# Two small steps of every layer norm move from GpSimd to VectorE in a four-layer graph kernel

## The chip, the cores and the metric

The kernel runs on one core of one Trainium2 chip. A core has TensorE (PE in the profile, with its weight loads apart as PEld), VectorE (DVE), ScalarE (ACT) and GpSimd (POOL), which work from queues of their own and meet by semaphores, and SyncE (SP), whose queue issues nearly all of the DMAs here. The metric is the time of one execution on the device, in microseconds (us); the run is judged by the median of several.

## The reference: four pre-norm graph layers

The input x holds 64 graphs of 256 nodes with 128 features, all with one 256 x 256 adjacency matrix. Every layer does `h = relu(layernorm(x))`, runs a graph layer on h and adds its result to x.

```python
def _layernorm(x, axis=-1, eps=1e-5):
    m = jnp.mean(x, axis=axis, keepdims=True)
    v = jnp.var(x, axis=axis, keepdims=True)
    return (x - m) / jnp.sqrt(v + eps)
...
pre = s1[:, :, None, :] + s2[:, None, :, :] + b_lin
h = jnp.where(pre >= 0, pre, ALPHA * pre)
e = jnp.einsum('bije,e->bij', h, a) + bias
attn = jax.nn.softmax(e, axis=2)
```

The lines from `pre` on are layer 0, the costly one: for every pair of nodes of a graph 256 numbers are made, passed through a leaky relu and summed with weights. Layer 1 is a gated sum over neighbours with two dense steps, layer 2 an attention masked by the adjacency matrix, layer 3 a gated recurrent unit of five steps.

The layer norm is done on all 128 features of a node, so mean and variance are two numbers per node. As nodes lie on the partitions, they are two columns per block of 128 nodes. The kernel never makes the normalized values by themselves: ScalarE computes `relu(rstd * x + shift)` in one instruction, with `rstd = (variance + epsilon) ** -0.5` and `shift = -mean * rstd`.

## The kernel before

**Tiles and groups.** The 64 graphs go in 34 groups: one graph each in the first two and the last two, two graphs in the others (`GROUPS`). A graph is two blocks of 128 nodes, so a group's x is a tile `xt` of 128 partitions by G blocks of 128 features, with G = 2 or 4.

**The layer norm** is `ln_relu` (L445 to L481), and every group goes through it four times, once per layer, 136 times in all. VectorE makes the statistics of each block (`bn_stats`, L457, into `bst`) and joins them (`bn_aggr`, L460, into `bmv`, which holds mean and variance side by side per block). Then GpSimd does four instructions on tiles of G columns: `bve` = variance + epsilon (L465), `bmm` = -mean (L466), `brs` = `bve` to the power -0.5 (L468) and `bsh` = `bmm` x `brs` (L470). Then ScalarE makes h, block by block (L477), with `bsh` and `brs` as its bias and scale. The generator yields the name of an engine ahead of each step; what stands between two yields is queued on that engine in one go.

**The pair stage** of layer 0 is most of the work. For each graph, `Pairs` makes buffers `r` of 128 x 4 x 2 x 256, in which a tile of 256 columns is the maximum of s2 and one column of -s1. Three engines make such tiles, each in its own form: ScalarE (L720, a relu with a bias), GpSimd (L725, one tile per instruction, all in SBUF) and VectorE (L702, four or eight tiles in one instruction, s2 read from PSUM and s1n from SBUF). A full buffer is a batch; TensorE sums it with the weights into `e_ps` (L786), and the buffer is free again. There are 12 buffers. When five or more batches wait for TensorE, the planner "merges": VectorE adds two buffers into one (L744, a maximum and a sum in one instruction), so that TensorE gets three batches in place of four.

**The order of the work** is set when the kernel is built, by a planner in the last part of the function. It keeps a clock for each of the four engines (`Model`), to which every instruction adds a price written in the code: a tile 365 ns on ScalarE and 454 on GpSimd, a VectorE instruction of the pair stage 1131, 2198 or 392, and for small ones

```python
def dve(n, pointers=0, more=0):
    model.op("dve", 66 + n * 1.042 + 60 * pointers + more)
    return nc.vector
def pool(ns):
    model.op("pool", ns)
    return nc.gpsimd
```

At each turn it takes the piece of work that can start first by these clocks: a step of one of the chains (layer norms and dense layers of other groups, each a generator), a batch for TensorE, a merge, or tiles for an engine that is free. A step that follows one on another engine may start 150 to 300 ns after it (`LAG`), and 100 ns more for most (300 for TensorE) while chains are paced. So a change of one price changes the order of nearly all of the program, and how many tiles each engine is given. On the chip every engine keeps the order it was given, whatever the instructions take in fact.

**Other places that the prediction speaks of.** At the start some constants are made on VectorE: L252 to L274 put the attention weights into order, L338 to L340 work on columns of two (`left`, `left_n`, `left_nb`), L442 adds two biases. L815 is the reciprocal of layer 0's softmax. L800 joins scores with adjacency and takes a minimum, L870 is layer 1's elu.

Of the kernel before, what the change touches and what calls it, by code (L numbers as in the profile page):

```python
# [8 lines left out]
F32 = mybir.dt.float32  # L9
AF = mybir.ActivationFunctionType  # L10
ALU = mybir.AluOpType

P = 128
N = 256
GROUPS = (1, 1) + (2,) * 30 + (1, 1)
LN_EPS = 1e-5
# [49 lines left out]
def kernel(ctx: ExitStack, tc: tile.TileContext, ins: dict, out: bass.AP):  # L66
# [9 lines left out]
    sp = ctx.enter_context(tc.tile_pool(name="small", bufs=3))  # L76
# [31 lines left out]
# [4 lines that stand above are left out]
    def act(n, pointers=0, sbuf=0, table=0, more=0):  # L112
        model.op("act", 50 + n * 0.832 + 69 * sbuf + (0, 75, 154)[pointers] + 11 * table + more)
        return nc.scalar
# [4 lines that stand above are left out]
# [329 lines left out]
    def ln_relu(space, xt, tag, ln, when=None, at=None, across=False):  # L448

        G = xt.shape[1]  # L450
        for g in range(G):
            if g % 2 == 0:
                yield "dve", when, at
            if g == 0:
                st = sp.tile([P, G, 6], F32, tag=tag + "_st", name="bst", bufs=1)
                mv = sp.tile([P, G, 2], F32, tag=tag + "_mv", name="bmv", bufs=1)
            dve(P).bn_stats(st[:, g, :], xt[:, g, :])  # L457
        yield "dve"
        for g in range(G):
            dve(6, more=15).bn_aggr(mv[:, g, :], st[:, g, :])  # L460
        yield "pool"

        ve = sp.tile([P, G], F32, tag=tag + "_ve", name="bve", bufs=1)
        minus = sp.tile([P, G], F32, tag=tag + "_mm", name="bmm", bufs=1)
        pool(277).tensor_scalar(ve, mv[:, :, 1], 1.0, LN_EPS, ALU.mult, ALU.add)  # L465
        pool(150).tensor_scalar(minus, mv[:, :, 0], -1.0, 0.0, ALU.mult, ALU.add)  # L466
        rstd = sp.tile([P, G], F32, tag=tag + "_rs", name="brs", bufs=1)
        pool(1085).tensor_tensor(rstd, ve, neg_half[:, 0:G], ALU.pow)  # L468
        shift = sp.tile([P, G], F32, tag=tag + "_sh", name="bsh", bufs=1)
        pool(302).tensor_tensor(shift, minus, rstd, ALU.mult)  # L470
        for g in range(G):
            if g % 2 == 0:
                yield "act"
            if g == 0:
                shape = [P, P, G] if across else [P, G, P]
                h = space.tile(shape, F32, tag=ln, name=tag, bufs={ap: 3, bp: 1}.get(space))
            act(P, 2, 1).activation(  # L477
                h[:, :, g] if across else h[:, g, :], xt[:, g, :], AF.Relu, bias=shift[:, g : g + 1],
                scale=rstd[:, g : g + 1],
            )  # L480
        return h  # L481
# [15 lines left out]
    def first_head(xt, to, snd):  # L497

        G, _, W = sizes(xt)
        h = yield from ln_relu(ap, xt, "h0", "h0", at=LANDS)  # L500
        h_t = yield from transpose_blocks(ap, h, "h0t", psum_h)
        to.update(h=h, h_t=h_t)
        yield "pe", lambda: counts["w_p"] > 1
        s2_ps, s1_ps = psum_h([P, 2, N], "s2_ps"), psum_a([P, 2, W], "s1_ps")
        for half, p in ((1, s2_ps), (0, s1_ps)):
            for ec in range(2):
                mm(
                    p[:, ec, :], lhsT=w_p[:, half, bass.ts(ec, P)], rhs=flat(h_t),
                    start=True, stop=True,
                )  # L510
        yield "dve"
        s1n = ap.tile([P, 2, W], F32, tag="s1n", name="s1n")
        for ec in range(2):
            dve(W, 1).tensor_scalar(
                s1n[:, ec, :], s1_ps[:, ec, :], -1.0, blin_n[:, ec : ec + 1], ALU.mult, ALU.add
            )
        yield "act"
        s2 = ap.tile([P, 2, N], F32, tag="s2", name="s2")
        act(2 * N).copy(s2, s2_ps)
        s1 = ap.tile([P, 2, W], F32, tag="s1", name="s1")  # L520
        for ec in range(2):
            act(W, 1, more=27).activation(
                s1[:, ec, :], s1_ps[:, ec, :], AF.Identity, bias=blin_p[:, ec : ec + 1]
            )
        to.update(s1=s1, s1n=s1n)
        snd.update(s2=s2, s2_ps=s2_ps)

    def head(xt, to):
        G, _, W = sizes(xt)
        h = yield from ln_relu(ap, xt, "h0", "h0")  # L530
        h_t = yield from transpose_blocks(ap, h, "h0t", psum_h, settled)
        to.update(h=h, h_t=h_t)
        if counts["left"] > 0:
            yield from bounds(to)
        for ec in range(2):
            yield "pe", lambda: counts["w_p"] > 0
            p = psum_h([P, W], "s1_ps")
            mm(
                p, lhsT=w_p[:, 0, bass.ts(ec, P)], rhs=flat(h_t), start=True, stop=True
            )  # L540
            yield "act", lambda: counts["w_p"] > 1
            if ec == 0:
                s1 = ap.tile([P, 2, W], F32, tag="s1", name="s1")
                s1n = ap.tile([P, 2, W], F32, tag="s1n", name="s1n")
            act(W, 1, more=27).activation(s1[:, ec, :], p, AF.Identity, bias=blin_p[:, ec : ec + 1])
            yield "act"
            act(W, 1, more=27).activation(
                s1n[:, ec, :], p, AF.Identity, bias=blin_n[:, ec : ec + 1], scale=-1.0
            )
        to.update(s1=s1, s1n=s1n)  # L550
# [432 lines left out]
    def layer2(x2, by_memory):  # L983
        G, NB, W = sizes(x2)
        h = yield from ln_relu(bp, x2, "h2", "h", across=True)
        if by_memory:
            h_t, at = crossed(h, "h_t", "h_t", "act")
# [484 lines left out]
```

## Time and profile before

| | |
|---|---|
| median of 3 runs | 4956.28 us (4955.85 to 4961.9) |
| profiled execution, its own time | 4962.75 us |
| its span, first to last instruction | 4960.9 us |
| granted TensorE clock, mean | 0.999 |
| instructions on VectorE, GpSimd | 8229, 10545 |
| GpSimd tiles, L725 | 9920, busy 4509.6 us, 543 ns each |
| ScalarE tiles, L720 (main group) | 9768, busy 4421.0 us, 1212 ns each |
| VectorE, L702 whole and half | 761 at 2277 ns, 606 at 1210 ns |
| VectorE merges, L744 | 4056 at 472 ns |
| statistics, L457 and L460 | 512 at 278 ns, 512 at 153 ns |

A profile comes from one execution, taken by the hardware profiler. In its groups the first number after the bar is the time in which at least one instruction of the group ran, then the mean time of one, then the idle time of the engine just before them with what ended most of it. Instructions of one engine overlap: a tile of ScalarE shows 1212 ns, yet 9768 of them fit in 4421.0 us. So the time that one more instruction adds to a full engine is less than the time it shows, and is read from runs of equal instructions. TensorE's busy time is modelled, and an engine that is busy in the profile may still wait inside. The last 161 us, after 4800, are a tail in which the last groups end their chains and the makers of tiles have little left.

### The profile page before, as it was taken

To read this page: it belongs to the slowest core of one execution; us is meant where nothing else is said; L and a number is where in the kernel's file an instruction comes from. 1 tells how busy PE (TensorE), PEld (TensorE's weight loads), DVE (VectorE), ACT (ScalarE), POOL (GpSimd) and SP (SyncE) were. 2 spreads that over 40 slices of the span, in tenths; PEclk is the share of its full clock that TensorE was granted. 3 is DMA by queue.
4 is the path that set the end of the run, shared out by engine and by line. 5 is a ranking of instruction groups with operands and counts; after the bars stand their busy time and mean duration, and the time that the engine had idled before them with its cause. 6 is when DMAs were issued, how large, how long until landed. Compare 5 with 4: busy or idle time off the path is not lost.

```text
span 4960.9 us, 176723 instructions
## 1 busy us (share of the span) xinstructions
PE 4923.5 (99%) x69735; PEld 2389.7 (48%) x69735; DVE 4841.8 (98%) x8229; ACT 4873.2 (98%) x12812; POOL 4756.8 (96%) x10545
## 2 busy tenths in 40 slices
PE   9999999999999999999999999999999999999998
PEld 4454545554454544444445444444454444444444
DVE  9999999999999999999999999999999999999994
ACT  8999999999999999999999999999999999999994
POOL 8999999999999999999999999999999999999981
PEclk9999999999999999999999999999999999999999
DMA  0357576777676776866757656656666555542310
GB/s 21 10 17 23 25 30 27 32 32 30 30 33 27 32 32 28 34 27 30 33 27 30 30 27 32 32 26 32 30 32 32 26 31 30 29 26 12 19 9 8
DMA packets 3431090, 132.92 MB, mean 27 GB/s; under 512 B 3369201, under 2 KB 3405937, under 8 KB 3430257
## 3 DMA queue, kind: packets, MB, share of 16 engines
q1 hardware_dynamic: 3429712, 121.35, 56.5%
q8 instruction: 547, 8.96, 0.9%
q14 instruction: 287, 2.34, 0.3%
q10 hardware_dynamic: 544, 0.26, 0.0%
HBM read 61.48 MB, written 60.10 MB: 25 GB/s over the span
## 4 chain that ended last, share of the span: by engine, by line
PE 85%; ACT 7%; DVE 5%; POOL 1%; issue 1%; DMA 0%; ACTq 0%; DVEq 0%; POOLq 0%
PE e_ps L786 53%; PE gate_ps L128 8%; PE hv_ps L128 5%; ACT r L720 5%; PE m_ps L128 5%; PE s_ps L128 3%; DVE r L702 3%; PE o_ps L128 2%; PE e_ps L128 2%; PE rc_ps L128 1%; POOL r L725 1%; PE rsum_ps L128 1%; DVE r L744 1%; PE e_ps L135 1%; PE th_ps L128 1%
## 5 line engine op out<-in xcount | busy, mean ns | idle before, releaser
L725 POOL TENSOR_SCALAR r<-s,s1n 128x256 f32<-128x256 f32 x9920 | 4509.6, 543 | 47.1 <-PE e_ps L786 21.1
L720 ACT ACTIVATE r<-s_act,s 128x256 f32<-128x256 f32 x9768 | 4421.0, 1212 | 1.1 <-PE e_ps L786 1.0
L786 PE MATMUL e_ps<-r,a_win 128*32 128x256 f32 (+1 forms) x41040 | 3323.2, 464 | 9.1 <-DVE r L702 7.5
L702 DVE TENSOR_TENSOR r<-s_ps,s1n 128x2048 f32<-128x2048 f32 (+1 forms) x1367 | 2417.3, 1804 | 0.0
L786 PEld LDWEIGHTS e_ps<-r,a_win 128*32 128x32 f32 x41040 | 1394.2, 110 | 1603.7 <-issue 825.0
L744 DVE SCALAR_TENSOR_TENSOR r<-s_ps,s1n,r 128x256 f32<-128x256 f32 x4056 | 1671.5, 472 | 0.8 <-POOL r L725 0.3
L477 ACT ACTIVATE h<-xt,bsh,brs 128x128 f32<-128x128 f32 x512 | 417.6, 1318 | 7.5 <-POOL bsh L470 7.5
L720 ACT ACTIVATE r<-s,s 128x256 f32<-128x256 f32 x512 | 319.2, 1416 | 0.0
L128 PE MATMUL m_ps<-adj_q,hn 128*32 128x256 f32 x4096 | 252.1, 380 | 1.6 <-ACT hn L1140 1.6
L128 PEld LDWEIGHTS m_ps<-adj_q,hn 128*32 128x32 f32 x4096 | 160.8, 132 | 89.4 <-issue 25.4
L1192 ACT ACTIVATE gate_ps<-gate_ps,bz 128x512 f32<-128x512 f32 (+1 forms) x140 | 202.5, 1447 | 0.0
L1194 ACT ACTIVATE hv_ps<-hv_ps,bh 128x512 f32<-128x512 f32 (+1 forms) x140 | 200.9, 1435 | 0.0
L1180 ACT ACTIVATE m_ps<-gate_ps,br 128x512 f32<-128x512 f32 (+1 forms) x140 | 194.0, 1386 | 0.0
L1176 ACT COPY m_t<-m_ps 128x512 f32<-128x512 f32 (+1 forms) x140 | 184.7, 1319 | 0.0
L128 PE MATMUL gate_ps<-m_t,t_w_w 128*32 128x512 f32 (+1 forms) x1360 | 174.8, 568 | 0.4 <-ACT m_t L1090 0.3
L128 PE MATMUL hv_ps<-rh,u_th 128*32 128x512 f32 (+1 forms) x1360 | 170.9, 567 | 1.3 <-DVE rh L1103 1.3
L128 PE MATMUL gate_ps<-m_t,w_t 128*32 128x512 f32 (+1 forms) x1360 | 171.1, 568 | 0.6 <-ACT m_ps L1100 0.6
L128 PE MATMUL hv_ps<-m_t,t_w_w 128*32 128x512 f32 (+1 forms) x1360 | 171.0, 567 | 0.0
L809 ACT ACTIVATE pm<-e_ps,nmax 128x256 f32<-128x256 f32 x128 | 145.7, 1138 | 2.4 <-DVE nmax L800 2.4
L128 PE MATMUL gate_ps<-hf,u_t 128*32 128x512 f32 (+1 forms) x1088 | 139.8, 567 | 0.0
L128 PE MATMUL s_ps<-h0t,w_p 128*32 128x256 f32 (+1 forms) x1568 | 138.9, 445 | 0.6 <-ACT h0t L493 0.5
L940 ACT ACTIVATE th_ps<-th_ps,a_src 128x256 f32<-128x256 f32 x128 | 134.8, 1053 | 1.5 <-PE th_ps L128 1.5
(223 smaller groups left out, 4612.8 us busy)
## 6 DMA issues: line engine op xcount, KB each, us to landing
there<-hf SPq DMA_DIRECT2D x104, 256.0 KB
hn<-there SPq DMA_DIRECT2D x104, 256.0 KB
there<-h SPq DMA_DIRECT2D x86, 256.0 KB
h_t<-there SPq DMA_DIRECT2D x60, 256.0 KB
xt<-in_x_dram SPq DMA_DIRECT2D x30, 256.0 KB
out_dram<-xt SPq DMA_DIRECT2D x30, 256.0 KB
h3t<-there SPq DMA_DIRECT2D x26, 256.0 KB
row<-rows SPq DMA_DIRECT2D x128, 0.5 KB
```

Source lines behind the costliest of these rows:

```text
L128: nc.tensor.matmul(out[bass.ts(c, 32)], lhsT=lhsT[:, bass.ts(c, 32)], rhs=rhs, **flags)
L477: act(P, 2, 1).activation(h[:, :, g] if across else h[:, g, :], xt[:, g, :], AF.Relu, bias=shift[:, g : g + 1], scale=rstd[:, g : g + 1],)
L702: nc.vector.tensor_tensor(r[:, 2 * g2 : 2 * g2 + n, :, :], s2[:, ec : ec + 1, :].unsqueeze(1).to_broadcast([P, n, 2, N]), s1n.to_broadcast ...
L720: nc.scalar.activation(r[:, g, ic, :], s2[:, ec, :], AF.Relu, bias=s1[:, ec, i : i + 1])
L725: nc.gpsimd.tensor_scalar(r[:, g, ic, :], s2[:, ec, :], FLT_MAX, s1n[:, ec, i : i + 1], ALU.min, ALU.max,)
L744: nc.vector.scalar_tensor_tensor(r[:, g, ic, :], self.own("dve")[:, 1, :], self.of["s1n"][:, 1, i : i + 1], r[:, g, ic, :], ALU.max, ALU.add,)
L786: nc.tensor.matmul(to, lhsT=a_win[:, sign, 31 - t : 63 - t], rhs=of, start=False, stop=self.over, skip_group_check=True,)
L809: act(N, 1, more=119).activation(pm[:, ic, :], e_ps[:, ic, :], AF.Exp, bias=nmax[:, ic : ic + 1], scale=-1.0, accum_out=rs[:, ic : ic + 1],)
L1176: act(W).copy(m_t, m_ps)
L1180: act(W, 1).activation(m_ps, g_ps, AF.Tanh, bias=br, scale=0.5)
L1192: act(W, 1).activation(g_ps, g_ps, AF.Tanh, bias=bz, scale=0.5)
L1194: act(W, 1).activation(hv_ps, hv_ps, AF.Tanh, bias=bh)
```

## The change

The sum of variance and epsilon, which GpSimd made, is made by VectorE, right behind the aggregates and in the same step. The negative mean is no longer made. GpSimd does the power alone, at its old price of 1085. Then the chain goes back to VectorE for a step of its own, in which one instruction makes the shift out of mean, -1 and `rstd`. The chain of engines in a layer norm was VectorE, GpSimd, ScalarE; it is VectorE, GpSimd, VectorE, ScalarE.

```diff
@@ ln_relu
         yield "dve"
         for g in range(G):
             dve(6, more=15).bn_aggr(mv[:, g, :], st[:, g, :])
+        ve = sp.tile([P, G], F32, tag=tag + "_ve", name="bve", bufs=1)
+        dve(G).tensor_scalar(ve, mv[:, :, 1], 1.0, LN_EPS, ALU.mult, ALU.add)
         yield "pool"
 
-        ve = sp.tile([P, G], F32, tag=tag + "_ve", name="bve", bufs=1)
-        minus = sp.tile([P, G], F32, tag=tag + "_mm", name="bmm", bufs=1)
-        pool(277).tensor_scalar(ve, mv[:, :, 1], 1.0, LN_EPS, ALU.mult, ALU.add)
-        pool(150).tensor_scalar(minus, mv[:, :, 0], -1.0, 0.0, ALU.mult, ALU.add)
         rstd = sp.tile([P, G], F32, tag=tag + "_rs", name="brs", bufs=1)
         pool(1085).tensor_tensor(rstd, ve, neg_half[:, 0:G], ALU.pow)
+        yield "dve"
         shift = sp.tile([P, G], F32, tag=tag + "_sh", name="bsh", bufs=1)
-        pool(302).tensor_tensor(shift, minus, rstd, ALU.mult)
+        dve(G).scalar_tensor_tensor(shift, mv[:, :, 0], -1.0, rstd, ALU.mult, ALU.mult)
         for g in range(G):
             if g % 2 == 0:
                 yield "act"
```

In the changed kernel the sum is L462, the power L466 and the shift L469; lines from L477 on stand one lower (L702 is L701, L720 is L719, L725 is L724, L744 is L743, L786 is L785).

## The prediction

> **What bounds the kernel now.** I read the page's busy shares and its chain of work first, then the busy time by stretch, then the groups kept apart by shape.
>
> ```profile
> PE 4923.5 (99%) x69735; PEld 2389.7 (48%) x69735; DVE 4841.8 (98%) x8229; ACT 4873.2 (98%) x12812; POOL 4756.8 (96%) x10545
> PE 85%; ACT 7%; DVE 5%; POOL 1%; issue 1%; DMA 0%; ACTq 0%; DVEq 0%; POOLq 0%
> ```
>
> ```profile
> 100.00:4800.00 4700.00, 4690.85 (x66507) 2280.72 (x66508) 4659.67 (x7900) 4694.95 (x12358) 4623.27 (x10234) 1.00 0.61 28
> 4800.00:4961.00 161.00, 143.71 (x1970) 68.27 (x1960) 91.58 (x208) 90.84 (x222) 47.62 (x112) 0.97 0.02 7
> ```
>
> The second fence gives, per stretch, its length and then the busy time of PE, PEld, DVE, ACT and POOL. In the 4700 us body no engine rests: VectorE is idle 40.3 us of it (0.9%), GpSimd 76.7, the others under 10. That is the planner's doing: it hands each free engine the next tiles of the pair stage, so four engines fill up together. Work taken from one engine is therefore not time won; it is spread by the planner, and the end goes to whichever engine has most work in fact. A price in the planner that is too low makes its engine the late one. The question is what the two moved instructions cost on VectorE, against what the planner thinks.
>
> **What leaves GpSimd.** From the groups by shape (mean ns of one, then idle before):
>
> ```profile
> L468 POOL TENSOR_TENSOR brs<-bve,neg_half 128x4 f32<-128x4 f32 x120 | 122.4, 1020 | 0.0
> L470 POOL TENSOR_TENSOR bsh<-bmm,brs 128x4 f32<-128x4 f32 x120 | 24.1, 201 | 9.4
> L466 POOL TENSOR_SCALAR bmm<-bmv 128x4 f32<-128x4 f32 x120 | 23.4, 195 | 10.1
> L465 POOL TENSOR_SCALAR bve<-bmv 128x4 f32<-128x4 f32 x120 | 23.3, 195 | 23.7 <-DVE bmv L460 15.4
> ```
>
> Each of the three small ones is 0.20 us plus a gap of some 0.08, as one norm in order of time shows: its instructions start at 2071.20, 2071.48, 2071.63 and 2072.73, the tile before ends at 2071.12, and two tiles after end at 2073.98. Less two tiles of 0.454 the block costs 1.95 us. The power alone, with a gap at each side, is 0.08 + 1.02 + 0.11 = 1.21. So 0.74 us goes per norm (0.84 if all three gaps go), times 136 norms = 101 us (to 114).
>
> **What the planner does with it.** The listing of the two built programs shows the change does what it says: 136 + 136 small instructions come to VectorE, 408 small ones on GpSimd become 136. It also shows how the pair stage is dealt anew: GpSimd 9920 to 10088 tiles; ScalarE's main tile group 9768 to 9712; VectorE's whole halves 761 to 726, half ones 606 to 652, merges 4056 to 4040; TensorE two batches more. Nothing else changes in number. Prices: a GpSimd tile is 4509.6/9920 = 0.454 us. Run on run, VectorE's instructions begin about 0.08 before the last one ends (five L744 took 2.05 us, not 5 x 0.472), so 2.20, 1.13 and 0.39 us. ScalarE: sixteen L720 took 6.80 us at 1.21 each, so 0.37. A batch on TensorE is 0.86 in the chain.
> - GpSimd: -101 + 168 x 0.454 = -101 + 76 = **-25 us** (to -38).
> - ScalarE: -56 x 0.37 = **-21 us**.
> - TensorE: **+1.7 us**.
> - VectorE: -35 x 2.20 + 46 x 1.13 - 16 x 0.39 = -77 + 52 - 6 = **-31 us**, before the 272 added ones.
>
> **What the added instructions cost.** The planner books 66 + 4 x 1.042 = 70 ns each, 19 us in all. The nearest rows are the kernel's own small VectorE instructions:
>
> ```profile
> L338 DVE TENSOR_SCALAR left<-left,odd_all 128x2 f32<-128x2 f32 x1 | 0.4, 429 | 0.0
> L339 DVE TENSOR_SCALAR left_n<-left 128x2 f32<-128x2 f32 x1 | 0.4, 420 | 0.0
> L340 DVE TENSOR_TENSOR left_nb<-left_n,c_L_gnn_b_lin 128x2 f32<-128x2 f32 x1 | 0.4, 406 | 0.0
> ```
>
> ```profile
> L442 DVE TENSOR_TENSOR bz<-c_L_gnn_w_b,c_L_gnn_u_b x1: 143/143/143, 103.1 to 103.1; 128x1 f32<-128x1 f32 x1
> L442 DVE TENSOR_TENSOR br<-c_L_gnn_w_b,c_L_gnn_u_b x1: 257/257/257, 103.4 to 103.4; 128x1 f32<-128x1 f32 x1
> L442 DVE TENSOR_TENSOR bh<-c_L_gnn_w_b,c_L_gnn_u_b x1: 348/348/348, 103.7 to 103.7; 128x1 f32<-128x1 f32 x1
> ```
>
> ```profile
> L815 DVE RECIPROCAL rh<-rs x64: 144/153/166, 98.2 to 4868.3; 128x2 f32<-128x2 f32 x64
> ```
>
> The first three read and write SBUF only and took 406 to 429 ns for two elements, while GpSimd ran tiles; the same forms took 128 to 160 at 3.6 to 5.7 us, with GpSimd in no instruction (L261 0.13, L271 0.16, L252 0.15). They began at 31.02, 31.49 and 31.94 us, so they ended at 31.45, 31.91 and 32.35: one GpSimd tile (0.454) apart. The L442 ones, two SBUF tensors each, took anything from 143 to 348. I read: such an instruction waits out the tile that GpSimd is in. A reciprocal of the same size does not: 64 times, never over 166. The new sum is of L339's kind and the new shift of L340's (two SBUF tensors). Through the body GpSimd is in a tile nearly always, and the main VectorE work avoids this, since it takes one operand from PSUM.
>
> With any remainder of a tile equally likely: 29% of the time it is under 130 ns and the instruction takes its 150; else the remainder plus 20, on average 0.31. Mean 266 ns. The sum also reads what the last aggregate has just written, and the listing gives it a wait on VectorE's own semaphore: 35 ns of gap (L271 ended 5.64, L272 began 5.67) in place of the 0.08 overlap. So:
> - sum: 35 + 266 = 301 ns (185 without the tile, 464 at worst)
> - shift: 266 - 81 = 185 ns (74 to 325)
> - per norm 486 ns, times 136 = **66 us** (35 to 107), 47 over the planner's 19.
>
> In L338 to L340 GpSimd lost nothing: six tiles around them took 2.79 us, which is 5 x 0.452 + 0.53. I add nothing to GpSimd.
>
> The Trainium skill, GPSIMD Engine Reference, Engine selection, speaks for the change: elementwise work belongs on VectorE, with GpSimd about twice as slow. By it alone the added pair would be half of what GpSimd takes, an estimate of 0.2 us a norm or 27 us, and VectorE would end at -4. Its page SBUF — State Buffer, Who interferes with whom, says that whoever starts first holds the shared port pair and the other blocks wholly; read to the letter GpSimd would lose some 0.15 us for each added instruction as well, an estimate of 41 us, which the tile spacing above does not show.
>
> **The sum.** VectorE gets -31 + 66 = **+35 us**; ScalarE and GpSimd get 21 to 25 lighter; TensorE stays. VectorE becomes the late engine, and what is late next is TensorE, which takes the batches in a fixed order and waits for VectorE's. Behind each added instruction stand VectorE's tiles and merges, so the delay reaches every batch that needs one. Cover: VectorE's 40.3 us of idle time in the body. Its named waits there sum to 35 us and are for others (7.9 for L786 before L800, 6.8 for L870, 4.9 for the products of layer 2); a VectorE that is behind finds these done. I let half of it go: 35 - 17 = **+18 us**. No cover would make it +35, full cover 0. The shift also waits for the power; a late VectorE finds it done, so I book nothing, and the gap to the worst price holds it. No DMA is issued by, or queued behind, the moved instructions: all but two loads of the start go by SP. In the last 161 us the norm's chain trades two GpSimd steps for a VectorE step and a hop, within 1 us either way per norm.
>
> The profiled execution took 4962.75 us (span 4960.9 and 1.85 around it), 6.5 above the median of the runs, 4956.28. The sum is a difference on the former, 4981; carried to the median it is **4974 us**.
>
> **Rivals.**
> - *Cover holds* (28%). The tile's remainder is mostly short, or the idle time takes all: VectorE -31 + 35 = +4 under 40 us of idle time. TensorE keeps its work and is busy 4690.85 of the body's 4700, so the end stays with it: about 4956. For it: the 64 reciprocals. Against: they have another form.
> - *Faster* (10%). TensorE's weight loads for the pair stage sat idle 88.7 us until a GpSimd tile and 79.0 until a ScalarE tile. Both engines get lighter by 0.4 to 0.5%. If those waits are real and a tenth goes, with VectorE's pair at 260 ns a norm: -17, so 4939. It decides once the pair costs under some 0.3 us. Against: each such wait is 0.3 us beside running matmuls.
> - *Worse* (12%). The waits line up with a tile's start, as in L338 to L340, where one wait set the phase of the next, or the shift stands waiting for a late power: 107 us. -31 + 107 - 20 = +56, so 5012.
> - The forecast has 50%.
>
> **How the numbers follow.** The forecast's own span, from half the idle time used to none of it, and prices a little to each side, is 4962 to 4990. Leaving out half of the faster case and half of the worse one, 4946 to 5008 holds eight in ten. 0.2% is 10 us, about what a measurement of this kernel can tell from no change. Faster by more: the faster case and a little of the cover case, 0.12. Within: most of the cover case and the low edge of the forecast, 0.30. Slower: 0.58.
>
> **What would show it.** In the changed profile the new L462 and L469 on VectorE should average 250 to 300 ns, spread from 150 to 430; L466 on GpSimd should stay near 1020 in 136; VectorE's idle time in the body should fall under 30 us and its waits for PE and ACT shrink, while TensorE's loads wait more for L701 and L743, and GpSimd waits more for `bve`. Both new lines at 150 would break the price; a VectorE as idle as now would break the bound; L469 waiting long for `brs` is the worse case.

## The result and the profile after

The changed kernel takes 4962.5 us (median of 20), the kernel before 4955.94 (of 20): a ratio of 1.0014, interval 1.0008 to 1.002, or **6.6 us more**. It is slower, by less than the 0.2% that I had named as the line.

The first profile of the kernel before came from an execution 6 us above its own median, so I compare with a second profile of that kernel (e5 below): spans of 4952.7 and 4959.3 us differ by 6.6, as the medians do. Each profile is one execution, and executions of one kernel differ by 2 to 6 us, so differences of 1 or 2 us between profiles say little. First the second profile of before, busy shares and the body (after the length: PE, PEld, DVE, ACT, POOL), then the same lines of after:

```profile
PE 4916.1 (99%) x69735; PEld 2370.3 (48%) x69735; DVE 4839.9 (98%) x8229; ACT 4864.2 (98%) x12812; POOL 4737.0 (96%) x10545
```

```profile
100.00:4800.00 4700.00, 4691.39 (x66608) 2264.72 (x66610) 4666.16 (x7925) 4694.14 (x12377) 4610.59 (x10250) 1.00 0.61 28
```

```profile
PE 4916.2 (99%) x69767; PEld 2323.5 (47%) x69767; DVE 4871.5 (98%) x8496; ACT 4851.6 (98%) x12756; POOL 4736.7 (96%) x10305
```

```profile
100.00:4800.00 4700.00, 4684.08 (x66500) 2213.19 (x66496) 4686.11 (x8144) 4673.49 (x12300) 4604.27 (x10012) 1.00 0.61 28
```

VectorE is busy 31.6 us more and idle 25.0 less (span less busy time: 112.8 to 87.8); the difference is the 6.6 us. In the body it rests 13.9 us in place of 33.8. ScalarE's busy time falls by 12.6 and its idle time rises from 88.5 to 107.7: the tiles taken off it bought nothing. GpSimd's busy time is unchanged, since 168 more tiles fill what three small instructions left; of the gaps that went with these nothing came back, for it now waits for VectorE. The new groups of after, and GpSimd's wait for the sum in the body:

```profile
L469 DVE SCALAR_TENSOR_TENSOR bsh<-bmv,brs 128x4 f32<-128x4 f32 x120 | 43.2, 360 | 0.7 <-POOL brs L466 0.6
L462 DVE TENSOR_SCALAR bve<-bmv 128x4 f32<-128x4 f32 x120 | 27.6, 230 | 4.1
```

```profile
POOL brs L466 <- DVE bve L462: 53.4, 59, 2.3
```

In the second profile of before the wait in the same place, of `bve` for `bmv`, was half of that:

```profile
POOL bve L465 <- DVE bmv L460: 27.3, 39, 1.8
```

VectorE hardly waits for anyone now, and TensorE waits more for it. Its longest waits in the body, after (`left_ps` is a smaller product of layer 0):

```profile
PE e_ps L785 <- DVE r L701: 7.1, 14, 1.6
PE left_ps L128 <- DVE r L701: 5.7, 7, 1.6
```

and in the second profile of before:

```profile
PE e_ps L786 <- DVE r L702: 5.1, 13, 1.2
PE left_ps L128 <- DVE r L702: 1.7, 4, 0.8
```

All such waits of TensorE in the body sum to 7.8 us there and to 15.2 after. The last matmul of the pair stage begins at 4867.4 us, not 4857.8: +9.6; the tail behind it is 3.0 us shorter. The chain of work that ended last (of each step, what released it) has moved from TensorE towards VectorE. Its shares in the second profile of before, in after, and in e4, an experiment below that only adds work to VectorE and keeps the order of before:

```profile
PE 88%; DVE 6%; ACT 4%; issue 1%; POOL 0%; DMA 0%; DVEq 0%; ACTq 0%; POOLq 0%
```

```profile
PE 59%; DVE 35%; issue 2%; ACT 2%; POOL 1%; DMA 0%; DVEq 0%; POOLq 0%; ACTq 0%
```

```profile
PE 75%; DVE 19%; ACT 5%; issue 2%; POOL 0%; DMA 0%; DVEq 0%; ACTq 0%
```

### The profile page after: what moved, and what is told of

It reads as the page before. It is cut to its first block, busy times and chain, and to the rows that moved or that the text cites. A ratio compares the mean times of both kernels' runs of the same rounds, so it can differ in the third digit from the quotient of the medians.

```text
span 4959.3 us, 176765 instructions
## 1 busy us (share of the span) xinstructions
PE 4916.2 (99%) x69767; PEld 2323.5 (47%) x69767; DVE 4871.5 (98%) x8496; ACT 4851.6 (98%) x12756; POOL 4736.7 (96%) x10305
## 4 chain that ended last, share of the span: by engine, by line
PE 59%; DVE 35%; issue 2%; ACT 2%; POOL 1%; DMA 0%; DVEq 0%; POOLq 0%; ACTq 0%
PE e_ps L785 36%; DVE r L701 17%; DVE r L743 11%; PE gate_ps L128 5%; PE hv_ps L128 4%; PE m_ps L128 4%; PE s_ps L128 2%; ACT r L719 1%; PE e_ps L128 1%; PE o_ps L128 1%; POOL r L724 1%; PE rc_ps L128 1%; DVE bst L457 1%; PE rsum_ps L128 1%; DVE rh L1196 1%
## 5 line engine op out<-in xcount | busy, mean ns | idle before, releaser
L724 POOL TENSOR_SCALAR r<-s,s1n 128x256 f32<-128x256 f32 x10088 | 4563.2, 476 | 46.2 <-PE e_ps L785 26.7
L719 ACT ACTIVATE r<-s_act,s 128x256 f32<-128x256 f32 x9712 | 4075.9, 829 | 5.4 <-PE e_ps L785 5.1
L785 PE MATMUL e_ps<-r,a_win 128*32 128x256 f32 (+1 forms) x41072 | 3302.1, 465 | 9.5 <-DVE r L701 9.1
L701 DVE TENSOR_TENSOR r<-s_ps,s1n 128x1024 f32<-128x1024 f32 (+1 forms) x1378 | 2396.1, 1773 | 0.0
L785 PEld LDWEIGHTS e_ps<-r,a_win 128*32 128x32 f32 x41072 | 1340.4, 110 | 1633.0 <-issue 862.8
L743 DVE SCALAR_TENSOR_TENSOR r<-s_ps,s1n,r 128x256 f32<-128x256 f32 x4040 | 1665.7, 471 | 0.6 <-POOL r L724 0.4
L476 ACT ACTIVATE h<-xt,bsh,brs 128x128 f32<-128x128 f32 x512 | 328.1, 898 | 14.9 <-DVE bsh L469 14.4
L719 ACT ACTIVATE r<-s,s 128x256 f32<-128x256 f32 x512 | 276.9, 932 | 0.0
L466 POOL TENSOR_TENSOR brs<-bve,neg_half 128x4 f32<-128x4 f32 (+1 forms) x136 | 133.5, 982 | 124.9 <-DVE bve L462 110.5
L1191 ACT ACTIVATE gate_ps<-gate_ps,bz 128x512 f32<-128x512 f32 (+1 forms) x140 | 141.4, 1010 | 0.0
L1193 ACT ACTIVATE hv_ps<-hv_ps,bh 128x512 f32<-128x512 f32 (+1 forms) x140 | 139.5, 997 | 0.0
L1179 ACT ACTIVATE m_ps<-gate_ps,br 128x512 f32<-128x512 f32 (+1 forms) x140 | 136.7, 976 | 0.8 <-PE gate_ps L128 0.8
L457 DVE BATCH_NORM_STATS2 bst<-xt 128x6 f32<-128x128 f32 x512 | 121.1, 277 | 2.1 <-DMA xt<-in_x_dram 1.6
```

The source lines that it names most:

```text
L476: act(P, 2, 1).activation(h[:, :, g] if across else h[:, g, :], xt[:, g, :], AF.Relu, bias=shift[:, g : g + 1], scale=rstd[:, g : g + 1],)
L701: nc.vector.tensor_tensor(r[:, 2 * g2 : 2 * g2 + n, :, :], s2[:, ec : ec + 1, :].unsqueeze(1).to_broadcast([P, n, 2, N]), s1n.to_broadcast ...
L719: nc.scalar.activation(r[:, g, ic, :], s2[:, ec, :], AF.Relu, bias=s1[:, ec, i : i + 1])
L724: nc.gpsimd.tensor_scalar(r[:, g, ic, :], s2[:, ec, :], FLT_MAX, s1n[:, ec, i : i + 1], ALU.min, ALU.max,)
L743: nc.vector.scalar_tensor_tensor(r[:, g, ic, :], self.own("dve")[:, 1, :], self.of["s1n"][:, 1, i : i + 1], r[:, g, ic, :], ALU.max, ALU.add,)
L785: nc.tensor.matmul(to, lhsT=a_win[:, sign, 31 - t : 63 - t], rhs=of, start=False, stop=self.over, skip_group_check=True,)
```

## The experiments

**Which engine's time counts: unread work on VectorE, with the order kept.** Five kernels add instructions to the kernel before, or to the changed one, that nobody reads and that the planner does not price, so that the order of everything else stays. Three of them add aggregates:

```diff
+        spare = sp.tile([P, 4, 2], F32, tag="spare", name="spare", bufs=1)
+        for k in range(4):
+            nc.vector.bn_aggr(spare[:, k, :], st[:, k % G, :])
```

e4, on the kernel before:

> The kernel before with four more aggregates per norm on VectorE, written to a spare tile that nobody reads and not priced, so the order of all else stays. 544 x 0.066 = 36 us more for VectorE. Theory (VectorE has some 26 to 30 us of idle time that can be filled, and every us beyond shows): +6 to +12 us, 4962 to 4968. Rival (TensorE alone sets the end and VectorE has far more room): 0 to +3. Second rival (each us on VectorE shows at once): +36.

4962.69 (interval of the ratio 1.0005 to 1.0022), +6.6. The theory holds. In the body VectorE rests 13.0 us and TensorE's waits sum to 15.8, nearly as in the changed kernel (13.9 and 15.2). e9, eight of them:

> The kernel before with eight more unread, unpriced aggregates per norm on VectorE, 1088 x 0.066 = 72 us of work; by the runs so far some 62 us more busy time. Theory (VectorE's added busy time costs little until its idle time is gone and nearly all of itself after; points so far: 8 us cost 1.1, 17 cost 2.6, 30 cost 6.6, 49 cost 18.7): +30 to +40, 4986 to 4996. Rival (a fixed share of each added us, about 0.22, because TensorE has slack for the rest): +14, 4970.

4991.48 (1.0059 to 1.0084), +35.9: in the theory's range, and far from the rival's; but see below the table. e6, four on the changed kernel:

> The changed kernel with four more unread, unpriced aggregates per norm on VectorE, 36 us. Theory (the change has used up VectorE's idle time; 14 us of it are left in the body): +25 to +34 over the changed kernel, 4987 to 4996. Rival (TensorE sets the end and VectorE still has room): +6 as on the kernel before, 4966 to 4970.

4974.33 (1.0025 to 1.005), +18.7 on before and +11.8 on after: between the two. The dose was smaller than I had reckoned, since VectorE's busy time rose by 17.7 us and not 36. The four aggregates stand between the last aggregate and the sum, and behind them the sum costs less:

```profile
L465 DVE TENSOR_SCALAR bve<-bmv 128x4 f32<-128x4 f32 x120 | 21.7, 180 | 0.0
```

Its gap of 35 ns is gone too. That is a finding on the sum: much of its price is that it stands right behind what it reads.

**The wait for GpSimd's tile by itself.** e7 adds one product of two SBUF tensors per norm to the kernel before, e8 a reciprocal in its place.

```diff
+        spare = sp.tile([P, G], F32, tag="spare", name="spare", bufs=1)
+        nc.vector.tensor_tensor(spare, neg_half[:, 0:G], neg_half[:, 0:G], ALU.mult)   # e7
+        nc.vector.reciprocal(spare, neg_half[:, 0:G])                                  # e8
```

> The kernel before with one more unread, unpriced VectorE instruction per norm, a product of two tensors of 128 x G in SBUF that waits for nothing. Theory (it waits out GpSimd's tile): 250 to 350 ns each, about 136 x 0.23 = 31 us for VectorE, so +4 to +8 us, as the four aggregates gave. Rival (such an instruction costs the planner's 70 ns, 10 us in all): 0 to +2.

> The same with a reciprocal of the same size and place in place of the product. Theory (no wait for the tile): 150 ns shown, 70 added, 10 us in all, 0 to +2 us. Rival (every added instruction costs alike): as the product.

Min, median and max of each, e7 and then e8:

```profile
L462 DVE TENSOR_TENSOR spare<-neg_half x136: 118/134/1410, 3.9 to 4906.4; 128x4 f32<-128x4 f32 x120, 128x2 f32<-128x2 f32 x16
```

```profile
L462 DVE RECIPROCAL spare<-neg_half x136: 123/146/159, 3.9 to 4904.3; 128x4 f32<-128x4 f32 x120, 128x2 f32<-128x2 f32 x16
```

e7 took 4958.24 (0.9998 to 1.0016), e8 4956.7 (0.9993 to 1.0011): +2.6 and +1.1, which the intervals do not part from nothing. The forms do part: the reciprocal never passes 159 ns, the product reaches 1410. But its median is not above the reciprocal's, and its mean is 210 (128x4), not the 250 to 350 I expected: 45 of the 136 met GpSimd between instructions and took 118 to 142 ns; the 91 that began in a tile took 239 in the mean. These began anywhere in it, with a median of 217 ns of the tile left.

The runs that only add to VectorE's load make one curve, e6 in the order of the changed kernel and the others in that of before; the changed kernel is set beside it. Busy time is against the 4839.9 of the second profile, time against the before of the same call:

| | VectorE busy, us | time, us |
|---|---|---|
| e8, reciprocal | +7.6 | +1.1 |
| e7, product | +16.9 | +2.6 |
| e4, 4 aggregates | +29.8 | +6.6 |
| the change | +31.6 | +6.6 |
| e6, the change and 4 aggregates | +49.3 | +18.7 |
| e9, 8 aggregates | +63.4 | +35.9 |

The first 30 us cost a fifth of themselves. From 30 to 49 us the time rises by 12, some three fifths. The step to e9 is 17 us of time for 14 of VectorE's, more than VectorE's load can explain by itself. GpSimd's tiles were slower in e9's profile, by some 2 ns each. In e5 and then in e9:

```profile
L725 POOL TENSOR_SCALAR r<-s,s1n 128x256 f32<-128x256 f32 x9920 | 4487.6, 477 | 49.7 <-PE e_ps L786 21.2
```

```profile
L728 POOL TENSOR_SCALAR r<-s,s1n 128x256 f32<-128x256 f32 x9920 | 4510.4, 482 | 47.1 <-PE e_ps L789 20.1
```

That is 22.8 us more for the same tiles; e4 has 4487.5, as e5. Why they were slower, and how much of e9's time is due to it, no run shows. So the runs show that the cost of added work rises steeply once some 30 us are used, but not that all of it shows from there on.

**Parts of the change.** e2 moves the shift alone, e3 the sum alone.

```diff
e2, against the kernel before
-        pool(150).tensor_scalar(minus, mv[:, :, 0], -1.0, 0.0, ALU.mult, ALU.add)
-        pool(302).tensor_tensor(shift, minus, rstd, ALU.mult)
+        yield "dve"
+        dve(G).scalar_tensor_tensor(shift, mv[:, :, 0], -1.0, rstd, ALU.mult, ALU.mult)
e3, against the kernel before
+        dve(G).tensor_scalar(ve, mv[:, :, 1], 1.0, LN_EPS, ALU.mult, ALU.add)
         yield "pool"
-        pool(277).tensor_scalar(ve, mv[:, :, 1], 1.0, LN_EPS, ALU.mult, ALU.add)
```

> Only the shift is moved; the sum stays on GpSimd. Theory: VectorE gets 136 x 0.28 = 38 us, of which the planner knows 10; it takes some 15 us of pair work from VectorE for what GpSimd gives up, so VectorE nets about +20 us, under the 26 us of idle time that the change used up: 4953 to 4958. Rival (the second trip and its wait): as slow as the whole change, 4960 to 4965.

> Only the sum is moved; GpSimd still makes minus, power and shift, so there is no second trip. Theory: VectorE gets 136 x 0.265 = 36 us, the planner takes some 9 us of pair work back, net about +25, just at the idle time: 4955 to 4960. Rival (second trip): no slower than before, 4953 to 4957.

e2: 4959.18 (0.9997 to 1.0015), +3.1. e3: 4965.51 (1.0011 to 1.0028), **+9.4**, more than the whole change. Neither expectation fits. VectorE is busy only 3.4 us more in e2 and 19.8 in e3, so both lie above the curve. In e2 the last matmul of the pair stage begins at 4851.7, 6.1 before that of e5, and a longer tail takes it back. In e3 TensorE's waits in the body are 21.8 us, against 7.8; by far the most are for L702:

```profile
PE e_ps L786 <- DVE r L702: 9.9, 19, 1.5
PE left_ps L128 <- DVE r L702: 9.4, 8, 1.6
```

e12 keeps the change and gives the sum a step of its own.

```diff
             dve(6, more=15).bn_aggr(mv[:, g, :], st[:, g, :])
+        yield "dve"
         ve = sp.tile([P, G], F32, tag=tag + "_ve", name="bve", bufs=1)
```

> The changed kernel with a step of its own for the sum, so that other VectorE work stands between the last aggregate and the sum in 134 of 136 norms. Theory (most of the sum's cost is that it waits for the aggregate's result): the sum adds 100 to 190 ns in place of 265, VectorE's added busy time falls by 10 to 20 us: 4957 to 4961. Rival (the longer chain of steps of the norm is what costs): 4962 or more.

4973.83 (1.0025 to 1.005), +18.3. The time lies in the rival's range; the theory has its mechanism right and its forecast wrong: the added cost of the sum (128x4), measured from the end of the instruction before, falls from 265 ns to 163, VectorE's busy time is only 3.8 us under the changed kernel's, and the whole is 11.3 slower. Here the pair stage ends 11.6 later than in e5, TensorE waits 26.4 us, and the tail is 7 us longer. TensorE, VectorE and GpSimd are all busy less than in the changed kernel, ScalarE 4.4 us more. So the new order that the planner made seems worse in a way that no engine's load shows; whether it is the norm's longer chain, as the rival has it, no run tells.

**Prices and merges.** e1 gives the changed kernel the prices that its profile shows; e10 lets the kernel before merge from four waiting batches on; e11 does both to the changed kernel.

```diff
e1 and e11, against the changed kernel
-        dve(G).tensor_scalar(ve, mv[:, :, 1], 1.0, LN_EPS, ALU.mult, ALU.add)
+        dve(G, more=195).tensor_scalar(ve, mv[:, :, 1], 1.0, LN_EPS, ALU.mult, ALU.add)
-        dve(G).scalar_tensor_tensor(shift, mv[:, :, 0], -1.0, rstd, ALU.mult, ALU.mult)
+        dve(G, more=205).scalar_tensor_tensor(shift, mv[:, :, 0], -1.0, rstd, ALU.mult, ALU.mult)
e10 and e11
-SPARE = 5
+SPARE = 4
```

> The changed kernel with only the planner's prices raised to what its profile shows: 265 ns for the sum and 275 for the shift, in place of 70 each. Theory (VectorE is the late engine because its work was priced too low): the planner takes about 400 ns x 136 = 54 us of tiles off VectorE and spreads it, so the time falls by 6 to 12 us, to between 4950 and 4957. Rival (the time comes from the second trip to VectorE, the wait of the shift behind the power): the prices change nothing, 4960 to 4965.

4960.83 (1.0001 to 1.0018), +4.8. The number lies in the rival's range, but the rival's reason is not there: the shift waits 0.4 us for the power in the whole body. The theory's gain did not come either. VectorE is relieved, busy 26.4 us less than in the changed kernel and idle 38.7 us in the body. But against the kernel before the planner made 80 merges less, which give TensorE ten batches more, 8.6 us at 0.86; against the changed kernel it is eight batches.

> The kernel before, merging from four waiting batches on in place of five. By the two programs: 34 batches less on TensorE (34 x 0.86 = 29 us), VectorE 272 merges more, 30 whole and 29 half instructions less (+8 us), ScalarE +16, GpSimd +18. Theory A (TensorE's work and its waits set the end): -5 to -15 us. Theory B (VectorE alone sets the end): +1 to +3, as the 8 us of the reciprocal gave.

> The changed kernel with the true prices and merges from four waiting batches on. Against the priced one alone: 29 batches less on TensorE (25 us), VectorE +232 merges, -38 whole, +1 half (+8 us), GpSimd +40 tiles (18 us). If the priced one lost its time to the ten batches more that TensorE got (theory A), this one gains 5 to 12 on it: 4949 to 4956. Theory B (VectorE alone): 4961 to 4964.

4968.04 (1.0015 to 1.0036) and 4967.01 (1.0015 to 1.0032): +12.5 and +11.5. Theory A's gain did not come. TensorE got 34 and 19 batches less than the kernel before and the time rose; what rose with it is the makers' busy time, in e10 by 8.8 us on VectorE, 15.8 on ScalarE and 17.3 on GpSimd. Theory B does not give the size. TensorE's work does not set the time by itself here, and neither does VectorE's. A reading that fits is that all four engines stand so near the limit that taking from one and giving to another loses; it is not shown, as both kernels also have an order of their own. None of the runs is faster than the kernel before.

e5, the kernel before unchanged, profiled again:

> The kernel before, unchanged, profiled once more, since its first profile came from an execution some 6 us above its own median. Theory (TensorE's work and its waits set the end): TensorE stands idle in the body as long as in the first profile or less, 6 to 9 us, against 16 in the changed kernel; VectorE is idle 35 to 42 us. Rival (the first profile is not typical and the two kernels hardly differ): TensorE idle 12 us or more.

4954.56 us in its one run; TensorE waits 7.8 us, as the theory had it, VectorE is idle 33.8, a little under its range.

## Why the prediction was right, and what was off

The sign and the mechanism hold: VectorE became the late engine, its idle time paid for part of the new work, TensorE waits for its buffers, and what GpSimd and ScalarE were spared did not shorten the time. The size does not: the forecast was +18 us, the result +6.6. At 4962.5 us the result is just inside the forecast's own span of 4962 to 4990, and well inside the range of 4946 to 5008 by that range's width. Slower by more than 0.2%, to which I gave 0.58, did not come; within 0.2%, at 0.30, did.

- **The cover was mis-sized.** "I let half of it go: 35 - 17 = +18 us." 25.0 us of VectorE's idle time went, 19.9 of them in the body, not 17. This makes 8 of the 11.4 us that I was off, as an account: time is busy time plus idle time on any engine. The curve shows the same from load alone: of e4's 30 us of work on VectorE four fifths were covered. I also took the body's idle time from an execution that was not typical (40.3, where the second shows 33.8).
- **VectorE's load** was nearly right, 31.6 us for 35; that is the other 3.4. Part of this is luck. Without overlaps the two new instructions are busy 67 us, where I had 66 with the gaps before them; the pair work falls by 29 for my 31, and VectorE's other work takes 6 less, which I did not foresee. The two prices were off in opposite ways: with the gap before it the sum adds 264 ns, not 301, and the shift 275, not 185. The sum shows a mean of 230 ns, not 266, as in 73 of 136 norms it met no tile: GpSimd had come to the power and stood waiting for this very sum. One such norm in after, VectorE and then GpSimd (start, length, both in us):

```profile
1635.95 0.17 DVE L462 TENSOR_SCALAR bve<-bmv 128x4 f32<-128x4 f32 x1
```

```profile
1636.20 1.02 POOL L466 TENSOR_TENSOR brs<-bve,neg_half 128x4 f32<-128x4 f32 x1 [1.15 <-DVE bve L462]
```

  Those 73 took 168 to 172 ns. The shift shows 342 over all norms, not 266. My even spread of remainders left out that it can wait longer than a tile: seven of 136 took over 1 us, and without these seven the mean is 278.
- **What the others were spared.** I had GpSimd 25 us lighter and ScalarE 21; their busy time fell by 0.3 and 12.6.
- **What GpSimd loses: next to nothing.** Its tile adds 452 ns in the second profile of before and in the changed one. The Trainium skill, SBUF — State Buffer, Who interferes with whom, has either side block the other. Here VectorE waited for hundreds of ns, and GpSimd for tens at most: of the 160 tiles that ran beside e7's product, 16 added over 460 ns and none over 507, and beside e8's reciprocal none of 106 passed 456. In sum that is 0.4 us.
- **The added pair as "half of what GpSimd takes".** That factor stands in the skill's table for instructions with two inputs, and the sum has one. The measured pair was far from the 27 us worked out from it: with gaps the two add 0.54 us a norm on VectorE, about what the same two steps cost on GpSimd (0.40 us and two gaps of some 0.08).
- **"The shift also waits for the power; a late VectorE finds it done"**: 0.4 us of such waits in the body. Right.
- **The signs.** GpSimd's power stayed (median 1017 ns), VectorE's idle time in the body fell under 30 us, and GpSimd waits more for `bve`. But neither new line averaged 250 to 300 ns: at 128x4 the sum shows 230 and the shift 360, with longest ones of 1726 and 2189.
- **The tail** I held to within 1 us per norm; it is 3.0 shorter with three norms in it, at the edge of that.
- **The rivals.** *Cover holds*, at 4956, is nearer to the result than the forecast's 4974, but by other terms: not VectorE +4 under 40 us of idle time, but +31.6, of which 25 were covered. *Faster* and *worse* did not come.

What stays open: every kernel whose order the planner made anew and in which I could compare (e1, e2, e3, e10, e11, e12) lies some 3 to 12 us above the curve. The changed kernel has a new order as well and lies on the curve, so a cost of its order and a gain from the lighter GpSimd and ScalarE may cancel in it. That its 6.6 us come from VectorE's load alone is therefore likely, from e4 and the waits, but not shown. No run holds the order and moves only the two instructions.

## What to carry to other kernels

Where a planner keeps four engines full, an instruction moved from one to another is not worth its own time but the difference of two margins: ask first how much idle time the receiving engine has left, then whether the giver can use what it is spared. Here work up to that margin cost a fifth of itself, and beyond it most of itself, so measure the margin with unread instructions in a fixed order, which separates load from order. A change that also makes the planner deal anew carries several us either way that no sum over the instructions tells.

## What the runs showed of the hardware

- In these runs a VectorE instruction with two SBUF tensors that starts in a GpSimd tile mostly takes the rest of that tile and some 14 ns (the median of e7's products and of the shifts that outlast it). But it does not always get in at the tile's end. Seven of the 136 shifts took over 1 us; this one, of 2.19 us, stood while GpSimd ran tile after tile (VectorE, then GpSimd, in after):

```profile
1522.59 2.19 DVE L469 SCALAR_TENSOR_TENSOR bsh<-bmv,brs 128x4 f32<-128x4 f32 x1
```

```profile
1522.30 2.75 POOL L724 TENSOR_SCALAR r<-s,s1n 128x256 f32<-128x256 f32 x6
```

- The small sum, right behind the aggregate that makes its operand, adds some 205 ns in the median (a gap of 35, then 171) even with no tile in the way; in e6, with four unrelated aggregates between, it adds 54.
- A VectorE instruction that does not read the one before mostly begins some 80 ns before that one ends (82 in the median for the shift), so a row's mean overstates what one more instruction adds.
